# Two graph networks in one kernel: the division by relation counts and the mixtures placed two bases later, the counts' lower limit on ScalarE, and other PSUM banks in v2 and the output projection

## The chip, the cores and the metric

The kernel runs on one core of a Trainium2 chip, in 32-bit floating point throughout. The metric is the device time of one execution in microseconds; lower is better. TensorE is called PE here, VectorE DVE, ScalarE ACT, GpSimd POOL, and SyncE SP, as in the profile.

## The reference, cut to what matters

There are 384 nodes with 1024 features, and 12,672 edges.

```
h = relu(layernorm(x));  x = x + attention(h)      # 16 heads, mask from the edges
h = relu(layernorm(x));  x = x + relational(h)

attention: q, k, v = linear(h); q2, k2, v2 = linear(q), linear(k), linear(v)
           softmax(q2 k2^T / 8 + mask) v2, then a linear map (the output projection)
relational (D = 768, R = 6 relations, B = 4 bases, L = 2 layers):
  x = relu(h w_in + b_in)
  per layer:  W_r = sum_b comp[r,b] basis[b]
              out[n] = sum over edges (s -> n, type r) of (x W_r)[s] / counts[r, n]
                       + x root + bias
              x = batchnorm(relu(out) + x)
  layernorm(x w_out + b_out)
```

`counts[r, n]` is the number of edges of type r that end in n.

## The kernel before

**Edges to dense matrices.** POOL scatters edge values into tables in device memory: the mask values into `mtab` (L261) and the edge counts into `atab` (L266, an indirect DMA that adds). The four mask tables are read back and merged on DVE into the tile `mask8` (L306 to L320). These steps are a generator, `edge_steps`; `fill(n)` runs n steps of it between pieces of other work. The count tables are read into `A`, six relations of 384 x 384 (L830 to L837): two loads on SP and the rest on POOL, where a second table is accumulated into each relation by DMA. `add_up(r)` sums a relation's three row tiles on POOL.

**Attention.** After q, k and v, the product v2 is made in halves by `v_products`, a scheme with fewer multiplications and more additions, in banks of PSUM that `vbanks` names. The last third of the rows is made by `second_v(half)` (L562), which stands between the first score products (L701). `exponents(g)` reads the scores and `mask8` on DVE, then ACT takes the exponential. The output projection is at L789 to L826; its last rows are two plain products at L818 to L823, with `relu_T` (transposes of the normalised rows) between them.

**Relational layers.** For each layer and basis b, PE computes H_b = X basis_b (L950 to L992): three pieces c = 0, 1, 2, then products of sums (`times`), each read from PSUM by ACT or DVE. One product, `rest`, is left over and done after piece 0 of the next basis. Behind the four bases comes X root (L994 to L1001), then At times H (from L1057 on), where

    At_b = sum_r comp[r,b] * A_r / counts_r

`share(r)` (L340) divides: PE adds up `sums[r]` over the partitions with a matrix of ones (L343), DVE limits the count to at least 1, takes the reciprocal and multiplies `A[:, r]`; it then starts `add_up(r + 4)`. `mix(l, r, At, bs)` (L324) adds relation r into At for the bases `bs`, on ACT for r = 0 and on DVE otherwise. The table `between` (L932) says after which piece of which basis each is called: the key is (layer, basis, piece), where piece 4 is the end of a basis and basis 4 is the root product. Bases are counted from 0 here: the third and fourth are 2 and 3.

**What sets the order.** The order of every engine is that of the program (`manual_schedule`). PSUM has 8 banks, and `next_bank(name, among)` takes the bank that was handed out longest ago among those allowed:

```
i = next(i for i in ring if i in among)
ring.remove(i)
ring.append(i)
```

A product into a bank waits until what the bank held was read. Weights go through `wload`, five buffers and SP's queue. A basis needs three loads; the third of the next basis and two of the one after start as the current basis lets go of its buffers.

Of the kernel before, what the change touches and what calls it, by code (L numbers as in the profile page):

```python
# [10 lines left out]
F32 = mybir.dt.float32  # L11
# [6 lines left out]
P = 128  # L18
# [33 lines left out]
def gnn_kernel(ctx: ExitStack, tc: tile.TileContext, out, x, edges, chunks, cols, rows, small,  # L52
# [14 lines left out]
    def bank(i, name):  # L67
        return psum.tile([P, 512], F32, tag=f"bank{i}", name=name)

    def next_bank(name, among=range(8)):  # L70
# [4 lines that stand above are left out]
        return bank(i, name)  # L75
# [45 lines left out]
    nc.vector.tensor_scalar(ident, jp, 0.0, None, ALU.is_equal)  # L121
    ones = const.tile([P, P], F32, name="ones")
    nc.gpsimd.memset(ones, 1.0)

    hT = keep.tile([P, KD, N], F32, tag="hT", name="hT")

# [46 lines left out]
    def edge_steps(ep, none, zero):  # L173
# [129 lines left out]
        for i in range(EC - PER + DEALT):  # L303
            put_count()
            if i == 1:
                V = [mask8] + [ep.tile([P, NT, N], F32, tag=f"V{j}", name=f"V{j}") for j in range(1, MT)]  # L306
                for v, tab in zip(V, mtab):
                    nc.gpsimd.dma_start(v, tab[:MCELLS, :].rearrange("(t p d) o -> p t (d o)", p=P, t=NT))
                for j, v in enumerate(V[1:]):
                    if j == 1:  # L310
                        yield
                    given = ep.tile([P, NT, N], F32, tag="given", name="given")
                    nc.vector.tensor_scalar(given, v, 4.0 * NEG, None, ALU.is_gt)
                    nc.vector.copy_predicated(mask8, given.bitcast(I32), v)

                for n in range(NT):
                    blk = mask8[:, n, n * P:(n + 1) * P]
                    bare = ep.tile([P, P], F32, tag="bare", name="bare", bufs=2)
                    nc.vector.scalar_tensor_tensor(bare, blk, 4.0 * NEG, ident, ALU.is_lt, ALU.mult)
                    nc.vector.copy_predicated(blk, bare.bitcast(I32), sp[:, 2, 3:4].to_broadcast([P, P]))  # L320
# [10 lines left out]
                nc.vector.scalar_tensor_tensor(At[:, b], A[:, r], w, At[:, b], ALU.mult, ALU.add)  # L331

    sums = {}

    def add_up(r):
        sums[r] = late.tile([P, N], F32, tag="sum", name="sum", bufs=4)
# [2 lines left out]

    def share(r):  # L340

        ps = next_bank("ps_cnt", ring[1:])
        nc.tensor.matmul(ps[:, :N], ones, sums[r], start=True, stop=True)  # L343
        rn = late.tile([P, N], F32, tag="rn", name="rn", bufs=2)
        nc.vector.tensor_scalar(rn, ps[:, :N], 1.0, None, ALU.max)
        nc.vector.reciprocal(rn, rn)
        nc.vector.tensor_tensor(A[:, r], A[:, r], rn[:, None, :].to_broadcast([P, NT, N]), ALU.mult)
        if r + 4 < R:
            add_up(r + 4)


    with ExitStack() as inner:
# [68 lines left out]
        with tc.tile_pool(name="edge", bufs=1, side="right") as ep:  # L421
# [131 lines left out]

            v2 = ap.tile([P, NT, D], F32, tag="T", name="v2", bufs=4)
            VT = [output_weights(half) for half in range(2)]
            vbanks = [[bank(i, "ps_v2") for i in range(3)], [next_bank("ps_v2", (4, 5, 6, 7)) for _ in range(3)]]

            def v_out(half, i, j):
                c = half * 512 + j * 256
# [1 line left out]

            def second_v(half):  # L562

                ps = next_bank("ps_v2", (4, 5, 6, 7))
                for k in range(KD):
                    nc.tensor.matmul(ps, v[:, k, 2 * P:], wv2[half][k // 4][:, k % 4, :],
                                     start=(k == 0), stop=(k == KD - 1))
                return lambda: nc.scalar.copy(v2[:, 2, half * 512:(half + 1) * 512], ps)
# [4 lines left out]
            def v_products(half):  # L573

                pa, pb, pc = [ps[:, :256] for ps in vbanks[half]]
                T1, T2, T3, T4 = VT[half]
                multiply(pa, va(0, 0), vb(half, 0, 0), True)
                nc.scalar.copy(v_out(half, 0, 0), pa)
                yield
                multiply(pb, va(0, 1), vb(half, 1, 0), True)  # L580
                add_out(half, 0, 0, pb)
                yield
                multiply(pc, VS[0], T1, True)
                nc.scalar.copy(v_out(half, 1, 1), pc)
                yield
                multiply(pa, VS[1], T2)
                nc.scalar.copy(v_out(half, 0, 1), pa)
                yield
                multiply(pc, VS[3], vb(half, 1, 1))
                add_out(half, 0, 1, pc)  # L590
                yield
                pd = bank(3, "ps_v2")[:, :256] if half == 0 else next_bank("ps_v2", (4, 5, 6, 7))[:, :256]
                multiply(pd, va(1, 1), T4, True)
                multiply(pa, VS[2], T3)

                def last():
                    nc.scalar.copy(v_out(half, 1, 0), pa)
                    add_out(half, 1, 1, pa)
                    add_out(half, 1, 0, pd)

                yield last
# [5 lines left out]
            next(first)()  # L607
            for _ in range(3):
                next(second)
            fill(1)  # L610
            next(second)()
            fill(1000)
        late = ctx.enter_context(tc.tile_pool(name="late", bufs=1, side="right"))
        soft_stack = ExitStack()
        soft = soft_stack.enter_context(tc.tile_pool(name="soft", bufs=1, side="right"))
# [200 lines left out]
        T4 = keep.tile([P, 4, HN], F32, tag="mask8", name="T4")  # L816

        for j in range(2):  # L818
            ps = next_bank("ps_y")[:, :256]
            for k in range(KD):  # L820
                nc.tensor.matmul(ps, attT[:, k, 2 * P:], w_o[1][k // 4][:, k % 4, j * 256:(j + 1) * 256],
                                 start=(k == 0), stop=(k == KD - 1))
            add_y(2, 512 + j * 256, ps)  # L823
            if j == 0:
                for t in range(2):
                    relu_T(h2T, t, xn[:, t, :], (0, 1))  # L826
# [60 lines left out]
    with tc.tile_pool(name="conv", bufs=1) as cp:  # L887
# [38 lines left out]
        def shares(*rs):  # L926
            return lambda: [share(r) for r in rs]

        def mixes(l, r, *bs):
            return lambda: mix(l, r, At, bs)  # L930

        between = {(0, 1, 0): shares(0), (0, 1, 1): shares(1), (0, 1, 2): lambda: mix(0, 0, At),  # L932
                   (0, 1, 4): mixes(0, 1, 0, 1), (0, 2, 0): shares(2), (0, 2, 2): shares(3),
                   (0, 2, 4): mixes(0, 2, 0, 1), (0, 3, 0): shares(4), (0, 3, 1): shares(5),
                   (0, 3, 4): lambda: [mix(0, r, At, (0, 1)) for r in (3, 4, 5)],
                   **{(0, 4, r): mixes(0, r, 2, 3) for r in range(1, R)},
                   (1, 0, 0): mixes(1, 0, 0, 1, 2, 3)}
        for i in range(10):
            between[1, (i + 1) // 3, (i + 1) % 3] = mixes(1, 1 + i // 2, *((0, 1), (2, 3))[i % 2])
# [7 lines left out]
        for l in range(L):  # L947
# [2 lines left out]
            rest = lambda: None  # L950
            for b in range(B):
                hs = [[H_[:, b, n, i * HC:(i + 1) * HC] for i in range(2)] for n in range(NT)]
                pe, pf, pb, pc, pa = [next_bank("ps_g")[:, :N] for _ in range(5)]
                kept = ring[-2:]

                def times(ps, x, y, start=False):

                    for c in range(3):
                        nc.tensor.matmul(ps, x[:, c], y(c), start=start and c == 0, stop=(c == 2),  # L959
                                         skip_group_check=not start)  # L960

                for c in range(3):
                    for ps, n, i, o, first in ((pa, 0, 0, 0, True), (pe, 2, 0, 0, True), (pf, 2, 0, 1, True),
                                               (pb, 0, 1, 0, True), (pe, 2, 1, 0, False), (pf, 2, 1, 1, False)):
                        nc.tensor.matmul(ps, block(XT, n, i)[:, c], w[c][:, i, o * HC:(o + 1) * HC],  # L965
                                         start=(first and c == 0), stop=(c == 2 and (i == 1 or ps is pa)))
                    if c == 0:
                        rest()
                        T4 = last_sums(w, T[1])
                    go_between(l, b, c)  # L970
                nc.scalar.copy(hs[0][0], pa)
                nc.vector.tensor_tensor(hs[0][0], hs[0][0], pb, ALU.add)
                times(pc, S[:, 0], lambda c: T[0][:, c], True)
                nc.scalar.copy(hs[2][0], pe)
                nc.scalar.copy(hs[2][1], pf)
                nc.scalar.copy(hs[1][1], pc)
                times(pa, S[:, 1], lambda c: T[1][:, c])
                nc.scalar.copy(hs[0][1], pa)
                times(pc, S[:, 3], lambda c: w[c][:, 1, HC:])
                nc.vector.tensor_tensor(hs[0][1], hs[0][1], pc, ALU.add)  # L980
                times(pa, S[:, 2], lambda c: T[2][:, c])
                nc.vector.tensor_tensor(hs[1][1], hs[1][1], pa, ALU.add)

                def rest(pa=pa, X=XT, T4=T4, dst=hs[1][0]):
                    times(pa, block(X, 1, 1), lambda c: T4[:, c])
                    nc.scalar.copy(dst, pa)

                if b + 1 < B:
                    w = load_basis(l, b + 1)
                    T = weight_sums(w)  # L990
                go_between(l, b, 4)
# [249 lines left out]
```

## Time and profile before

| | |
|---|---|
| median of 3 runs (lowest, highest) | 738.69 us (736.06, 740.8) |
| the profiled execution: its own time | 741.77 us |
| its span, first to last instruction | 740.0 us |
| mean granted clock of PE in it | 0.984 |
| busy in the span: PE, DVE, POOL, ACT | 705.5, 519.0, 309.6, 150.6 us |
| instructions: PE, DVE, POOL, ACT | 3228, 1313, 236, 348 |
| output projection ends, first product of h2T | 357.88 us from the start |
| basis 0, 1, 2, 3 of layer 0 begin on PE | 387.7, 407.0, 440.8, 463.4 |
| root product of layer 0, then At H begin on PE | 486.0, 511.1 |

A line of a timeline gives the start in us, the duration, the engine, the line of the kernel, the operation, the tiles out<-in, how often, and in brackets the idle time before and what ended it. A matmul in 32-bit floats appears as two instructions. A line of waits gives who waited for whom, the total in us, how often, and the longest. A row of windows gives the stretch and its length, then the busy time of PE, weight load, DVE, ACT and POOL with counts, then the granted clock of PE (1 is full), the DMA engines' share and GB/s.

### The profile page before, as it was taken

Reading aid. Unit: us, or ns where it says so; the run is one execution under the profiler, and the core shown is the slowest. Engines: PE = TensorE matmul, PEld = TensorE weight load, DVE = VectorE, ACT = ScalarE, POOL = GpSimd, SP = SyncE. Lnnn points to the kernel's source line nnn. Section 1 sums busy time; section 2 is a strip of 40 time slices with the busy share of each in tenths; the row PEclk is TensorE's granted clock in tenths of the full one; section 3 lists DMA queues with packets and bytes.
Section 4 is the critical chain, followed back from the end, with each engine's and each line's share of the span. In section 5 each row is a group of like instructions: output and inputs, shape, how many; then the busy total and the mean of one; then the engine's idle time right before and its main releaser. Section 6 shows DMA issues by size and latency. Waiting matters only on the chain.

```text
span 740.0 us, 8821 instructions
## 1 busy us (share of the span) xinstructions
PE 705.5 (95%) x3228; PEld 530.0 (72%) x3228; DVE 519.0 (70%) x1313; ACT 150.6 (20%) x348; POOL 309.6 (42%) x236
## 2 busy tenths in 40 slices
PE   8999999999995999997999689999999999999995
PEld 8759999999983444476995355557995555579943
DVE  6877796869774799775524559989679776506755
ACT  4202112111110577410131031101113111001100
POOL 1466767866887677587786471000000000030000
PEclk9999999999998999998999899999999999999999
DMA  8797787256424522633424993241002223610001
GB/s 296 255 369 219 227 243 209 39 198 202 116 57 129 170 2 1 214 43 44 85 1 66 256 245 87 114 171 43 11 33 76 73 108 128 240 58 1 1 28 57
DMA packets 40536, 91.00 MB, mean 123 GB/s; under 512 B 19644, under 2 KB 27680, under 8 KB 36270
## 3 DMA queue, kind: packets, MB, share of 16 engines
q1 hardware_dynamic: 18478, 79.62, 30.7%
q0 software_dynamic: 21008, 8.42, 10.4%
q10 hardware_dynamic: 1008, 2.41, 0.8%
q8 instruction: 25, 0.41, 0.2%
q14 instruction: 17, 0.14, 0.1%
HBM read 79.27 MB, written 11.16 MB: 122 GB/s over the span
## 4 chain that ended last, share of the span: by engine, by line
PE 64%; POOL 17%; DMA 11%; issue 6%; DVE 1%; ACT 0%; DVEq 0%; POOLq 0%
POOL atab L266 13%; PE ps_c L1057 11%; PE ps_g L965 10%; PE ps_k L382 10%; PE ps_g L959 9%; DMA atab<-count,at 8%; PE ps_c L999 6%; PE ps_q L400 6%; PE ps_q L382 5%; PE ps_f L1163 4%; POOL mtab L261 3%; DMA A<-atab 2%; PE ps_v L382 2%; DMA x_sb<-in_x 1%; DVE st L136 1%
## 5 line engine op out<-in xcount | busy, mean ns | idle before, releaser
L266 POOL DMA_INDIRECT atab<-count,at x99 | 164.7, 1664 | 58.8 <-DMA atab<-count,at 34.4
L261 POOL DMA_INDIRECT mtab<-m_val,at x99 | 106.9, 1080 | 57.2 <-issue 26.8
L1150 POOL TENSOR_TENSOR x_sb<-x_sb,room 128x1024 f32<-128x1024 f32 x3 | 7.0, 2349 | 194.0 <-DMA room<-in_rows 194.0
L331 DVE SCALAR_TENSOR_TENSOR At<-A,small_sb,At 128x1152 f32<-128x1152 f32 x40 | 53.7, 1413 | 0.0
L959 PE MATMUL ps_g<-T,S 128*128 128x384 f32 x144 | 49.1, 486 | 0.0
L965 PE MATMUL ps_g<-w_c,XT 128*128 128x384 f32 x144 | 48.9, 494 | 0.0
L965 PE MATMUL ps_g<-w_c,XN 128*128 128x384 f32 x144 | 47.6, 486 | 0.0
L400 PE MATMUL ps_q<-hT,w_q 128*128 128x384 f32 (+1 forms) x160 | 41.8, 422 | 1.4 <-ACT hT L90 1.4
L965 PEld LDWEIGHTS ps_g<-w_c,XT 128*128 128x128 f32 x144 | 28.0, 195 | 19.7 <-issue 1.5
L959 PEld LDWEIGHTS ps_g<-T,S 128*128 128x128 f32 x144 | 27.4, 190 | 19.1
L965 PEld LDWEIGHTS ps_g<-w_c,XN 128*128 128x128 f32 x144 | 27.3, 190 | 18.8
L400 PEld LDWEIGHTS ps_q<-hT,w_q 128*128 128x128 f32 x160 | 28.5, 190 | 14.1 <-ACT hT L90 1.7
L1087 DVE TENSOR_TENSOR XN<-XN,ps_c 128x192 f32<-128x192 f32 x38 | 12.6, 349 | 34.4 <-ACT XN L1043 19.7
L1057 PE MATMUL ps_c<-At,H 128*128 128x192 f32 x216 | 36.4, 326 | 0.0
L1057 PEld LDWEIGHTS ps_c<-At,H 128*128 128x128 f32 x216 | 35.4, 190 | 0.5
L382 PE MATMUL ps_k<-T,S 128*128 128x192 f32 x192 | 35.2, 327 | 0.5 <-ACT k L498 0.5
L382 PEld LDWEIGHTS ps_k<-T,S 128*128 128x128 f32 x192 | 31.8, 190 | 0.8 <-ACT k L498 0.8
L1163 PE MATMUL ps_f<-w_out,XN 128*128 128x512 f32 (+1 forms) x84 | 31.1, 531 | 0.0
L250 DVE SCALAR_TENSOR_TENSOR same<-keys,key,weigh 128x128 f32<-128x128 int32 x99 | 28.0, 346 | 1.2 <-DVE same L250 1.2
L250 DVE SCALAR_TENSOR_TENSOR same<-cells,own,later 128x128 f32<-128x128 int32 x99 | 27.9, 348 | 0.4
L656 DVE CUSTOM_DVE_ANT_0 s<-ps_s,mask 128x384 f32<-128x384 f32 x48 | 24.5, 549 | 5.0 <-PE ps_s L643 4.8
L1163 PEld LDWEIGHTS ps_f<-w_out,XN 128*128 128x128 f32 x84 | 15.9, 190 | 14.9 <-issue 14.3
(295 smaller groups left out, 1418.9 us busy)
## 6 DMA issues: line engine op xcount, KB each, us to landing
w_c<-in_basis SPq DMA_DIRECT2D x24, 768.0 KB
atab<-zero SPq DMA_DIRECT2D x12, 576.0 KB
A<-atab POOLq DMA_DIRECT2D x10, 576.0 KB
w_c<-in_root SPq DMA_DIRECT2D x6, 768.0 KB
w_q<-in_wq SPq DMA_DIRECT2D x4, 1024.0 KB
w_q<-in_wiq SPq DMA_DIRECT2D x4, 1024.0 KB
w_k<-in_wk SPq DMA_DIRECT2D x4, 1024.0 KB
w_k<-in_wik SPq DMA_DIRECT2D x4, 1024.0 KB
```

The source lines that it names most:

```text
L250: nc.vector.scalar_tensor_tensor(same, row[:, n, :], mine[:, c:c + 1], times, ALU.is_equal, ALU.mult, accum_out=count[:, i, c:c + 1])
L261: nc.gpsimd.indirect_dma_start(mtab[c // PER][:, :], bass.IndirectOffsetOnAxis(at[:, 0, c:c + 1], 0), m_val[:, c:c + 1], None)
L266: nc.gpsimd.indirect_dma_start(atab[0 if i < 18 - DEALT else i % 2][:, :], bass.IndirectOffsetOnAxis(at[:, 1, c:c + 1], 0), count[:, 1, c: ...
L331: nc.vector.scalar_tensor_tensor(At[:, b], A[:, r], w, At[:, b], ALU.mult, ALU.add)
L382: nc.tensor.matmul(ps, a[:, k, :], b[:, k, :], start=start and k == 0, stop=(k == 3), skip_group_check=not start)
L400: nc.tensor.matmul(ps[o][:, c], wt_[:, k, o * P:(o + 1) * P], src[:, k, c], start=(k == 0 and c.start == 0), stop=(k == KD - 1 and c.stop ...
L656: nc.vector.tensor_tensor_reduce(s[j], ps[:, :N], mask8[:, t, :], -scale, 3.0e38, ALU.add, ALU.min, tops[:, j:j + 1])
L959: nc.tensor.matmul(ps, x[:, c], y(c), start=start and c == 0, stop=(c == 2), skip_group_check=not start)
L965: nc.tensor.matmul(ps, block(XT, n, i)[:, c], w[c][:, i, o * HC:(o + 1) * HC], start=(first and c == 0), stop=(c == 2 and (i == 1 or ps is ...
L999: nc.tensor.matmul(pr[o], w[k // 2][:, k % 2, o * P:(o + 1) * P], XT[:, k, :], start=(k == 0), stop=(k == KC - 1))
L1057: nc.tensor.matmul(ps, x[:, c], y[:, c], start=start and c == 0, stop=stop and c == 5, skip_group_check=True)
L1163: nc.tensor.matmul(p, XT[:, k, t * P:(t + 1) * P], w[k // 2][:, k % 2, c0:c1], start=(k == 0), stop=(k == KC - 1))
```

## The change

- The shares leave basis 1 of layer 0 for bases 2 and 3; all mixtures of r = 1 to 5 are made at the end of basis 3, and those of r = 0 in pairs behind share 2 and share 3.
- The limit of the counts at 1 is computed on ACT as relu(count - 1) + 1, with a new constant tile `minus`.
- `share` takes a bank that the current basis doesn't use (`taken`), and a basis doesn't take the bank of the `rest` before it.
- In v2 the second half's banks are fixed to 4, 5, 6 and 7, and `second_v` uses 5 and 6. The merging of the mask tables is no longer cut by a `yield`, and stands ahead of the last additions of v2.
- The first plain product of the output projection's last rows takes any bank but 0.

```diff
+    minus = const.tile([P, 1], F32, name="minus")
+    nc.gpsimd.memset(minus, -1.0)
...
-                for j, v in enumerate(V[1:]):
-                    if j == 1:
-                        yield
+                for v in V[1:]:
                     given = ep.tile([P, NT, N], F32, tag="given", name="given")
...
+    taken = []
...
     def share(r):
-        ps = next_bank("ps_cnt", ring[1:])
+        ps = next_bank("ps_cnt", [i for i in range(8) if i not in taken])
         nc.tensor.matmul(ps[:, :N], ones, sums[r], start=True, stop=True)
         rn = late.tile([P, N], F32, tag="rn", name="rn", bufs=2)
-        nc.vector.tensor_scalar(rn, ps[:, :N], 1.0, None, ALU.max)
+        nc.scalar.activation(rn, ps[:, :N], AF.Relu, bias=minus)
+        nc.scalar.activation(rn, rn, AF.Identity, bias=ones[:, 0:1])
         nc.vector.reciprocal(rn, rn)
...
-            vbanks = [[bank(i, "ps_v2") for i in range(3)], [next_bank("ps_v2", (4, 5, 6, 7)) for _ in range(3)]]
+            vbanks = [[bank(i, "ps_v2") for i in range(3)], [next_bank("ps_v2", (i,)) for i in (4, 5, 6)]]
...
-                ps = next_bank("ps_v2", (4, 5, 6, 7))
+                ps = next_bank("ps_v2", (5 + half,))
...
-                pd = bank(3, "ps_v2")[:, :256] if half == 0 else next_bank("ps_v2", (4, 5, 6, 7))[:, :256]
+                pd = bank(3, "ps_v2")[:, :256] if half == 0 else next_bank("ps_v2", (7,))[:, :256]
...
-            fill(1)
+            fill(1000)
             next(second)()
-            fill(1000)
...
-            ps = next_bank("ps_y")[:, :256]
+            ps = next_bank("ps_y", range(1, 8))[:, :256]
...
-        between = {(0, 1, 0): shares(0), (0, 1, 1): shares(1), (0, 1, 2): lambda: mix(0, 0, At),
-                   (0, 1, 4): mixes(0, 1, 0, 1), (0, 2, 0): shares(2), (0, 2, 2): shares(3),
-                   (0, 2, 4): mixes(0, 2, 0, 1), (0, 3, 0): shares(4), (0, 3, 1): shares(5),
-                   (0, 3, 4): lambda: [mix(0, r, At, (0, 1)) for r in (3, 4, 5)],
-                   **{(0, 4, r): mixes(0, r, 2, 3) for r in range(1, R)},
+        between = {(0, 2, 0): shares(0), (0, 2, 1): shares(1),
+                   (0, 2, 2): lambda: [share(2), mix(0, 0, At, (0, 1))],
+                   (0, 2, 4): lambda: [share(3), mix(0, 0, At, (2, 3))],
+                   (0, 3, 0): shares(4), (0, 3, 1): shares(5),
+                   (0, 3, 4): lambda: [mix(0, r, At) for r in range(1, R)],
                    (1, 0, 0): mixes(1, 0, 0, 1, 2, 3)}
...
-                pe, pf, pb, pc, pa = [next_bank("ps_g")[:, :N] for _ in range(5)]
+                pe, pf, pb, pc, pa = [next_bank("ps_g", [i for i in range(8) if i not in taken[-1:]])[:, :N]
+                                      for _ in range(5)]
+                taken[:] = ring[-5:]
```

## The prediction

> **What bounds the kernel now.** I read the page's busy rows first: PE is at work in 95% of the span of 740.0 us (705.5), the next engine, DVE, in 70%. So only PE's idle time can be won, and the waits of PE alone list nearly all of it.
>
> ```profile
> PE ps_cnt L343 <- POOL sum L338: 8.9, 2, 6.9
> PE ps_v L566 <- DVE v L571: 7.9, 1, 7.9
> PE ps_y L821 <- DVE x_sb L784: 4.4, 1, 4.4
> PE ps_q L400 <- ACT hT L90: 1.4, 1, 1.4
> ```
>
> Three waits hold 21.2 us, and the change touches exactly these three. Next the windows around them; the first column after POOL is PEclk, the granted clock.
>
> ```profile
> 236.00:238.00 2.00, 1.83 (x2) 0.84 (x3) 1.97 (x4) 0.78 (x1) 0.55 (x1) 0.50 0.08 9
> 348.00:350.00 2.00, 2.00 (x6) 1.61 (x5) 0.00 (x0) 0.00 (x0) 1.69 (x2) 0.50 0.25 0
> 420.00:423.00 3.00, 3.00 (x5) 1.79 (x6) 1.33 (x2) 0.00 (x0) 0.00 (x0) 0.50 0.73 274
> ```
>
> After each of the three waits PE runs at half clock, so a wait costs more than its idle time. The timelines of PE, DVE, ACT and POOL show what must be ready:
>
> ```profile
> 346.59 6.26 PE L821 MATMUL ps_y<-w_o,attT 128*128 128x256 f32 x16 [4.40 <-DVE x_sb L784]
> ...
> 354.43 3.62 PE L821 MATMUL ps_y<-w_o,attT 128*128 128x256 f32 x16
> ```
> ```profile
> 233.37 0.96 DVE L313 TENSOR_SCALAR given<-V 128x1152 f32<-128x1152 f32 x1 [9.49 <-DMA V<-mtab]
> ...
> 242.79 0.56 DVE L656 CUSTOM_DVE_ANT_0 s<-ps_s,mask 128x384 f32<-128x384 f32 x1 [0.18 <-DVE mask L320]
> ...
> 486.61 21.35 DVE L331 SCALAR_TENSOR_TENSOR At<-A,small_sb,At 128x1152 f32<-128x1152 f32 x16
> ```
> ```profile
> 427.55 4.69 ACT L329 ACTIVATE At<-A,small_sb 128x1152 f32<-128x1152 f32 x4 [14.04 <-DVE A L347]
> ```
> ```profile
> 452.50 1.00 POOL L337 TENSOR_TENSOR sum<-A 128x384 f32<-128x384 f32 x1 [8.93 <-DMA A<-atab]
> ```
>
> The same 16 matmuls of L821 take 6.26 us after the wait and 3.62 without. The mask is the other thing to see: DVE gets the mask tables at 233.37 and can only begin the softmax at 242.79.
>
> **What the Trainium skill says.** "TensorE: Matmul & The Clock Gate", What's actually happening: the array falls to half clock after an idle window of some 3.4 us and needs about as long to come back. The trace agrees: 0.50 after idle times of 7.9, 4.4 and 6.9 us. The same page, Architectural detail, calls ACT's queue strictly first in, first out; the ACT timeline keeps program order. "ScalarE: Activation LUTs", Table sets: relu and identity are in every set, so the new activations should load no table; this trace has Relu and Identity side by side at L864 to L872 with no load. "DMA: Bandwidth & Descriptors", Queues, rings and completion order: the engines share themselves between the queues by packets. The trace agrees in that the accumulate into A issued at 438.5 landed at 452.5 (14 us) with three weight loads (issued from 437.75) beside it, and the one of 428.3 at 436.5 (8 us) without.
>
> **The change part by part**, against the execution of 741.77 us (span 740.0 and 1.8 around it). It is 3.1 us above the median of the runs, 738.69; I take the sum off the median.
>
> *Output projection.* The first L821 product gets a bank other than 0 (by the ring, 2), which was read long ago. It starts when L695 ends, 342.2, not at 346.59, and takes 3.5 us at full clock: done 345.7. The ring then gives bank 0 to the first transpose of relu_T, which waits for the addition that ends at 346.54: 0.9 us. Transposes 1.75 to 348.4, second product 3.5 to 351.9, where before the next matmul (first_products) came at 357.88. **Minus 6.0.** DVE is ready: the last xn is normalised at 345.9.
>
> *v2.* second_v(0) takes bank 5, read long ago, so the wait of 7.9 before it goes. What is late next is the softmax. scores(2), just behind second_v(0) on PE, needs the banks that exponents(0) reads, and these need the mask. Moving the last v2 additions (0.73) behind the rest of the mask work only reorders DVE, so exponents(0) stays at 242.79. PE does second_v(0) from 228.3 to 235.4, then idles 8 us until 243.4 and is cold again: scores(2), scores(3) take up to 3 us instead of 1.6. second_v(1) comes between 245.2 (no cold) and 246.5 (all cold), before at 246.17. So between minus 0.9 and plus 0.4; I take **0**.
>
> *Shares leave basis 1.* From its first matmul at 407.03 to that of basis 2 at 440.79 are 33.8 us; basis 2 with two share products took 22.6, so a bare basis is 22.6 less 2 x 0.65 = 21.3. The two products are done later, so 33.8 - 21.3 - 1.3 = **minus 11.2**, of which 8.9 was idle and 2.3 the cold clock. This needs sums ready at the new places. PE is 6 ahead, so basis 1 begins at 401.2 and basis 2 at 422.5; share 0 comes at 428.4 (sum ready 419.9), share 1 at 433 (428.4), share 2 at 437.5 (432.5), share 3 at 448 (438.6), 4 and 5 at 455 and 460 (443.6, 454.6). Every sum is early by 4.6 us or more; that is the cover.
>
> *Lower limit on ACT.* It removes 6 DVE instructions of 0.55 and adds 12 on ACT of about 0.52 (row of L1090). ACT is busy 20%; the reciprocal starts some 0.5 us later each time, and no PE instruction waits for it: 0.
>
> *share(2), then two mixtures on ACT, at the end of the matmuls of basis 2.* Behind them on ACT stands the copy of pa (L971), and pa's next product waits for that copy. Let t be the end of those matmuls. The count product ends t+0.65, two activations t+1.8, two mixtures of 1.17 (4.69/4) t+4.2, the copy t+4.7. PE has only the count product and pc's (1.94) until t+2.6. **Plus 2.1.** Before, the four mixtures ran ahead of that point (427.55 to 432.2) and PE never waited. The pair after share(3) hides behind the next basis' first 3.9 us of matmuls.
>
> *Banks.* By the ring, share(4) gets the bank that rest() has just filled, so its product waits for one ACT copy of 0.48: **plus 0.7** with the hand-over. All other new banks were read long before.
>
> *Mixtures behind basis 3.* 20 on DVE now follow basis 3, before 16 (486.61 to 507.96, 1.334 each): 5.3 us more. After them come four sums of At, four of H and take(0,0), which frees the bank for PE's product of 520.84; take ended 517.03, a slack of 3.8. 5.3 - 3.8 = 1.5, **plus 1.6** with the hand-over. q(0,0) itself is in time: 18 mixtures end 24 us after basis 3, PE gets there after 25.2.
>
> Sum: -6.0 - 11.2 + 0 + 2.1 + 0.7 + 1.6 = -12.8. 738.7 - 12.8 = **725.9**.
>
> *Unknown: DMA.* In basis 1, part 2 of its weights is issued on SP only behind A's loads (402.08), so at about 403, no earlier than 1 us before now; it had landed by 410.6 and PE needs it at 410.9. The next three loads move from 437.75 to about 419.5, into the loads and accumulates of A. Taking over the 6 us (14 less 8) that an accumulate lost beside loads, share 2, with 4.6 of slack, would stall by 1.4; bounds 0 and 6 (all of it, repeated at share 1). I take 0, since the loads thereby leave the later accumulates alone.
>
> **Rivals.**
> 1. *All costs hidden*: ACT's mixtures and the longer DVE tail find slack that I don't see, and second_v(1) comes 0.9 earlier. -17.2 - 0.9 = -18.1: 720.6. Against it: the ACT order is fixed.
> 2. *Weights and accumulates collide* as bounded above, with a cold clock after the stall (up to 2.3): -12.8 + 6 + 2 = -5: 734.
> 3. *The sums become the bound* (the other side). POOL issues each accumulate only after the load before it, so a delay of 6 us could repeat at each of relations 2 to 5: sum 5 at 454.6 + 24 = 478.6 against a need at 460, a stall of 18.6 and 2 cold. -12.8 + 20.6 = +7.8: 746.5. It decides once sum 5 is later than about 472 (12.8 less the cold 2 beyond 460), three full delays. Against it: the three loads are one burst of 2.4 MB, gone in 6 us at the 386 GB/s of 420 to 422.
> 4. *The chain on POOL sets the end*: the page's chain runs through POOL's scatters until the first sum, so PE's gains before 420 would turn into waiting at share 0. That holds if share 0 stood where it was; it now comes 8.5 us after its sum. If this cover failed, 6.0 goes back and the shares' gain shrinks: about 738, no change.
>
> **How the numbers follow.** My forecast, net -9 to -16 (722.5 to 729.5): 0.60. Rival 1: 0.12. Rival 2: 0.17. Rival 3: 0.05. Rival 4: 0.06. 1% is 7.4 us, about what a measurement of this kernel can tell from no change. Faster by more: 0.60 + 0.12 + half of rival 2 = 0.80; within: half of rival 2 and rival 4 = 0.15; slower: 0.05. The range leaves out the fast end of rival 1 and rivals 3 and 4: 721 to 734; the likeliest case alone is 722.5 to 729.5.
>
> **What would show it.** In the new profile: the waits of PE no longer list L343 <- POOL sum; L821 has two equal groups of 3.5; L566 has no wait, but an idle time of about 8 appears at L643 <- DVE s; a wait of about 2 at L959 on ACT H L971 in basis 2; one of 1 to 2 at L1057 on DVE L1087 in layer 0; no table load at share. I am wrong if PE waits at L343 for POOL, at L965 for a weight load, or gains its 7.9 at v2 after all.

## The result, and the profile after

| | before | after |
|---|---|---|
| median (lowest to highest, runs) | 739.42 (736.06 to 740.8, 4) | 729.05 (727.74 to 731.59, 4) |
| profiled execution; its span | 741.77; 740.0 | 731.59; 729.8 |
| PE busy | 705.5 | 702.7 |

The ratio is 0.987, 95% interval 0.9826 to 0.9915: faster by 1.3%, some 10 us. In a later series the changed kernel was measured again beside the kernel before and gave 0.9913 (0.9872 to 0.9953), some 6 us. Medians here count every execution; the ratios leave out those more than 1.5% above the fastest of their kernel. In four profiles, called late ones below, PE was busy for 93 to 104 of the 120 us from 100 to 220, against 119 in the profile before; only waits behind that stretch are read from them.

The waits of PE in the changed kernel (who waited for whom, us in total, times, longest):

```profile
PE ps_s L646 <- DVE top L659: 7.9, 1, 7.9
PE ps_g L964 <- ACT H L976: 2.0, 1, 2.0
...
PE ps_g L970 <- DVE XN L1092: 1.1, 1, 1.1
PE ps_h L165 <- DVE x_sb L787: 1.0, 1, 1.0
PE ps_c L1062 <- DVE XN L1092: 0.8, 1, 0.8
PE ps_cnt L345 <- ACT H L991: 0.7, 1, 0.7
```

The waits of 8.9 and 4.4 are gone. The one of 7.9 is not: it stands at the score products (L646) and no longer at v2. Five waits of 0.7 to 2.0 are new. PE's timeline shows what each costs behind itself:

```profile
241.32 3.40 PE L646 MATMUL ps_s<-k,q 64*128 64x384 f32 x8 [7.86 <-DVE top L659]
244.65 8.07 PE L570 MATMUL ps_v<-w_v,v 128*128 128x512 f32 x16
...
341.18 3.62 PE L824 MATMUL ps_y<-w_o,attT 128*128 128x256 f32 x16
345.75 1.97 PE L165 MATMUL ps_h<-ident,xn 128*128 128x128 f32 x16 [0.95 <-DVE x_sb L787]
347.56 3.62 PE L824 MATMUL ps_y<-w_o,attT 128*128 128x256 f32 x16
...
441.05 3.89 PE L964 MATMUL ps_g<-T,S 128*128 128x384 f32 x6 [2.04 <-ACT H L976]
```

Eight score instructions take 3.40 behind the wait where they take 1.56 at full clock, and the second v2 product 8.07 where it takes 7.13. The output projection's two products are equal now, 3.62 each. At 441.05 six matmul instructions took 3.89, which take 2.10 everywhere else in this profile: half clock again, behind a wait of only 2.04. The windows there have the granted clock in the last column but two:

```profile
243.00:244.00 1.00, 1.00 (x5) 0.43 (x3) 1.00 (x3) 1.00 (x5) 0.98 (x1) 0.50 0.06 0
...
443.00:444.00 1.00, 1.00 (x3) 0.61 (x2) 0.27 (x1) 0.00 (x0) 0.66 (x1) 0.50 1.14 200
```

Basis 1 has no share product left and no wait. Its first matmuls and those of basis 2, before and after:

```profile
407.03 4.03 PE L965 MATMUL ps_g<-w_c,XT 128*128 128x384 f32 x12
...
440.79 4.03 PE L965 MATMUL ps_g<-w_c,XT 128*128 128x384 f32 x12
```
```profile
400.14 4.03 PE L970 MATMUL ps_g<-w_c,XT 128*128 128x384 f32 x12
...
421.43 4.03 PE L970 MATMUL ps_g<-w_c,XT 128*128 128x384 f32 x12
```

On DVE, the softmax and the mixtures behind basis 3:

```profile
240.71 0.55 DVE L659 CUSTOM_DVE_ANT_0 s<-ps_s,mask 128x384 f32<-128x384 f32 x1
...
473.44 26.67 DVE L332 SCALAR_TENSOR_TENSOR At<-A,small_sb,At 128x1152 f32<-128x1152 f32 x20
```

**Where the time went.** The softmax can start only when the mask is merged, and that moment moved from 242.79 to 240.71 in these two executions. POOL had issued the loads of the mask tables 2.0 sooner too (224.62 instead of 226.60), and the second profile of the changed kernel has the softmax at 244.93, later than before the change. So this 2.1 is taken for chance. From it to the end of the execution there are 741.77 - 242.79 = 499.0 us before and 731.59 - 240.71 = 490.9 after: minus 8.1. In the second profile, with the mask at 244.93, the time was 736.01: 491.1, the same. The stretches (from PE's timelines, start to start) sum to it:

| stretch | before | after | difference | predicted |
|---|---|---|---|---|
| softmax begins to scores(4) on PE | 10.45 | 11.94 | +1.5 | 0 |
| to first_products | 104.64 | 98.36 | -6.3 | -6.0 |
| from first_products through basis 0 to basis 1 | 49.15 | 49.13 | 0 | 0 |
| basis 1 | 33.76 | 21.29 | -12.5 | -12.5 |
| basis 2, with two more count products | 22.57 | 27.86 | +5.3 | +3.4 |
| basis 3 | 22.58 | 23.47 | +0.9 | +0.7 |
| root product to the product with T2 (pa) | 34.90 | 36.46 | +1.6 | +1.6 |
| to the first product of layer 1 | 31.20 | 32.54 | +1.3 | 0 |
| layer 1 and the end | 189.73 | 189.83 | +0.1 | 0 |

### The profile page after: what moved, and what is told of

Its sections match the earlier page's. It is cut to its first block, busy times and chain, and to the rows that moved or that the text cites. A ratio compares the mean times of both kernels' runs of the same rounds, so it can differ in the third digit from the quotient of the medians.

```text
span 729.8 us, 8833 instructions
## 1 busy us (share of the span) xinstructions
PE 702.7 (96%) x3228; PEld 527.9 (72%) x3228; DVE 514.3 (70%) x1307; ACT 157.7 (22%) x360; POOL 309.6 (42%) x237
## 3 DMA queue, kind: packets, MB, share of 16 engines
q0 software_dynamic: 21008, 8.42, 10.4%
## 4 chain that ended last, share of the span: by engine, by line
PE 71%; DVE 12%; DMA 6%; POOL 6%; issue 3%; ACT 2%; DVEq 0%; POOLq 0%; ACTq 0%
PE ps_g L970 13%; PE ps_g L964 10%; PE ps_c L1062 9%; PE ps_q L404 6%; PE ps_q L386 5%; PE ps_k L386 5%; PE ps_f L1168 4%; POOL mtab L264 4%; DVE At L332 4%; PE ps_y L386 3%; PE ps_c L1004 3%; DMA mtab<-m_val,at 3%; PE ps_x L386 3%; PE ps_o L691 2%; PE ps_s L646 2%
## 5 line engine op out<-in xcount | busy, mean ns | idle before, releaser
L964 PE MATMUL ps_g<-T,S 128*128 128x384 f32 x144 | 51.0, 500 | 2.0 <-ACT H L976 2.0
L1092 DVE TENSOR_TENSOR XN<-XN,ps_c 128x192 f32<-128x192 f32 x38 | 12.5, 349 | 30.8 <-ACT XN L1048 19.7
L646 PE MATMUL ps_s<-k,q 64*128 64x384 f32 x96 | 23.4, 559 | 7.9 <-DVE top L659 7.9
L985 DVE TENSOR_TENSOR H<-H,ps_g 128x384 f32<-128x384 f32 x8 | 4.4, 555 | 35.0 <-PE ps_g L964 35.0
```

Source lines behind the costliest of these rows:

```text
L646: nc.tensor.matmul(score[g][j][:, :N], q2[ho, hc, t * P:(t + 1) * P], k2[ho, hc, :], start=True, stop=True)
```

## The experiments

Each was timed beside the kernel before on its chip; "ratio" is to that. A difference below some 3 us can't be read from these times, so the verdicts on parts of that size rest on lines of the profiles.

**One part alone.** Three kernels take one part each, a fourth leaves one out.

```diff
# a_out_bank: the kernel before and
-            ps = next_bank("ps_y")[:, :256]
+            ps = next_bank("ps_y", range(1, 8))[:, :256]
# b_shares: the change without that line and without v2
# c_v2: the kernel before with the banks and the fill of v2
# d_no_v2: the change without these
```

> The kernel before with one edit: the first plain product of the output projection's last rows takes any bank but 0. Theory (gains before the shares count only if the shares no longer wait for POOL): first_products follows 6.0 us sooner behind the scores, but share 0, still in basis 1, waits for its sum, so the wait at L343 grows from 6.9 to some 13 and the time stays within 1 us of 739.4. Rival (the three gains are independent): minus 6.0, 733.4.

Measured: 739.14, ratio 0.9962 (0.9925 to 0.9999), some 3 us, between the two expectations. The profile is a late one: PE reached the first scores at 246.28 instead of 226.74. So late, it met sums that were ready, and there was no wait at L343 to grow. It still ended 5.0 us sooner than the profile of before (736.79 against 741.77): the lead that it lacked is what the kernel before spends on its waits for the mask and the sums. Its two products at L821 take 3.62 each. That the gain needs the shares to be free of POOL is neither shown nor refuted by this run: it holds only for executions in which PE is ahead of POOL. The times of this series speak for it: d_no_v2 is b_shares plus this same edit, and from 0.9959 to 0.9869 are 6.7 us (4.1 to 9.3), where the edit alone gave 2.8 (0.1 to 5.5). The two intervals overlap, so this is a sign and no proof. The profile shows something else:

```profile
426.27 2.10 PE L959 MATMUL ps_g<-T,S 128*128 128x384 f32 x6
429.91 2.20 PE L959 MATMUL ps_g<-T,S 128*128 128x384 f32 x6 [1.54 <-ACT H L971]
```

With the sums on time, the kernel before has a wait on ACT of its own, behind its four mixtures of relation 0 (in c_v2, late too, 2.11). The wait for the sums had covered it.

> The change without its bank in the output projection and without the v2 part: shares, mixtures, taken and the limit on ACT alone. Theory: minus 11.2 for the shares, plus 3.8 at the ACT mixtures (2.0 of wait and 1.8 at half clock), 0.8 for the bank of share 4, 1.6 for the mixtures' tail, 1.2 at the start of layer 1: minus 3.8, 735.6. Rival (the costs of these parts come from the other edits' earlier arrival): minus 11, 728.

Measured: 738.41, ratio 0.9959 (0.9934 to 0.9984), minus 3: the theory's number, and the rival's minus 11 is out. Its profile, a late one, has the waits of 2.0 (ACT), 1.1 (layer 1), 0.8 (mixtures' tail) and 0.7 (bank of share 4) of the whole change, so they belong to this part. The half clock that the theory put behind the first is not there:

```profile
472.56 2.20 PE L967 MATMUL ps_g<-T,S 128*128 128x384 f32 x6 [2.04 <-ACT H L979]
```

> The kernel before with the v2 part alone. Theory: PE's idle time of 7.9 us moves from in front of second_v(0) to in front of scores(2), and the half clock moves with it onto more work: from exponents(0) on DVE to scores(4) on PE it takes 11.9 us instead of 10.5. The end does not move (739.4 within 1 us), since share 0 waits for POOL all the same. Rival (the 7.9 are won): scores(4) comes 7 us sooner after exponents(0), about 3.5 us; the end may still not move.

Measured: 738.9, ratio 0.9995 (0.9968 to 1.0022). The end doesn't move, as expected; on the move of the idle time its profile, a late one, says nothing, since PE came to the first scores 28 us after that of before and did not wait for the mask.

> The changed kernel without its v2 part. Theory: exponents(0) to scores(4) goes back from 11.9 to 10.5 us and nothing later swallows it: 1.4 faster than the changed kernel, some 727.6. Rival (the v2 part is a small gain, or nothing): 729 to 730, and 11.9 stays.

Measured: 734.35, ratio 0.9869 (0.9844 to 0.9893), not to be told from the changed kernel: the interval is 3.6 us wide and the two expectations differ by 1.4 to 2.4. Its profile is a late one as well. Inconclusive. That v2 costs 1.5 is thus read from profiles alone, the two of the changed kernel and that of f_limit_dve against the one of before, and no run without the v2 part confirms it.

**The wait on ACT.** Two kernels take its two suspects apart.

```diff
# e_mix_early
-        between = {(0, 2, 0): shares(0), (0, 2, 1): shares(1),
-                   (0, 2, 2): lambda: [share(2), mix(0, 0, At, (0, 1))],
+        between = {(0, 2, 0): shares(0), (0, 2, 1): lambda: [share(1), mix(0, 0, At, (0, 1))],
+                   (0, 2, 2): shares(2),
# f_limit_dve
-        nc.scalar.activation(rn, ps[:, :N], AF.Relu, bias=minus)
-        nc.scalar.activation(rn, rn, AF.Identity, bias=ones[:, 0:1])
+        nc.vector.tensor_scalar(rn, ps[:, :N], 1.0, None, ALU.max)
```

> The changed kernel with the first two mixtures of relation 0 on ACT placed behind share 1 instead of share 2. Theory (the mixtures in front of the copy of pa cost a wait of 2.0 us and then 1.8 us of half clock): both go, the six matmuls after the copy take 2.1 again and not 3.9, basis 3 begins 3.8 sooner after basis 2; 3.8 less than the changed kernel, some 725.3. Rival (the half clock belongs to the place, not to the wait): the wait goes, the 3.9 stay, 2.0 less.

Measured: ratio 0.988 (0.9811 to 0.9949), too wide to tell; its profiled execution took 725.02. In it the twelve instructions are in one piece, at full clock:

```profile
433.58 0.81 PE L345 MATMUL ps_cnt<-sum,ones 128*128 128x384 f32 x2
434.23 4.05 PE L964 MATMUL ps_g<-T,S 128*128 128x384 f32 x12
```

From share 0 to share 4 are 24.71 us (424.55 to 449.26), in the changed kernel 28.69 (427.23 to 455.92): 4.0 less, the theory's 3.8. The half clock went with the wait; that it doesn't belong to the place is seen as well from b_shares, d_no_v2 and g_clear, which have the wait and no half clock.

> The changed kernel with the lower limit back on DVE, one instruction. Theory (of the wait on the copy of pa, 1.2 us are the two new activations in front of the mixtures): the wait of 2.0 shrinks to 0.8, and the mixtures' tail is as before the edit; 1 to 2.5 less than the changed kernel. Rival (DVE then falls behind by 0.55 a share): nothing won.

Measured: 726.48, ratio 0.9847 (0.9815 to 0.9879), beside 0.9913 for the changed kernel in the same series. The wait is gone altogether, not shrunk to 0.8. ACT's timeline shows why, first in the changed kernel, then in this one:

```profile
437.11 0.58 ACT L348 ACTIVATE rn<-ps_cnt,minus 128x384 f32<-128x384 f32 x1 [3.29 <-PE ps_cnt L345]
437.72 0.61 ACT L349 ACTIVATE rn<-rn,ones 128x384 f32<-128x384 f32 x1
438.24 2.39 ACT L330 ACTIVATE At<-A,small_sb 128x1152 f32<-128x1152 f32 x2
440.54 0.46 ACT L976 COPY H<-ps_g 128x384 f32<-128x384 f32 x1
```
```profile
432.08 2.40 ACT L330 ACTIVATE At<-A,small_sb 128x1152 f32<-128x1152 f32 x2 [5.56 <-DVE A L350]
434.39 0.46 ACT L975 COPY H<-ps_g 128x384 f32<-128x384 f32 x1
```

In the changed kernel the first new activation waits for the count product, and behind it the mixtures wait too, though their data were ready: DVE had done relation 0's division at 433.9, ACT stood idle for 3.29. With the limit on DVE nothing on ACT waits for the count, and the mixtures run 2.8 us ahead of the count product at 434.88. So it is not the time of the two activations (1.2) that costs 2.0 of wait, but that they hold up what stands behind them. Either edit alone takes the wait away: it needs both, the activations and two mixtures behind them in front of the copy. At the scores this profile has a wait of 4.39 with 3.40 and 8.09 behind it, the same price as behind 7.86.

**Layer 1.**

```diff
# g_clear
         for l in range(L):
+            taken.clear()
```

> The changed kernel with the list of taken banks emptied at the start of a layer. Theory (the list still names a bank of layer 0, so the first product of layer 1 gets the bank that DVE reads last): the wait of 1.1 at the first matmul of layer 1 goes, 1.2 less. Rival (it waits for the normalised data): the wait stays.

Measured: ratio 0.9896 (0.985 to 0.9942); profiled execution 726.49. The wait is gone:

```profile
534.81 2.11 PE L1063 MATMUL ps_c<-At,H 128*128 128x192 f32 x12
536.76 8.55 PE L971 MATMUL ps_g<-w_c,XN 128*128 128x384 f32 x26
```

So layer 1 waited because `taken` still named a bank from layer 0: the ring passed over that one, and the first product got the bank that DVE had read last. The same profile has the ACT wait of 2.04 without half clock behind it:

```profile
438.97 2.20 PE L965 MATMUL ps_g<-T,S 128*128 128x384 f32 x6 [2.04 <-ACT H L977]
```

Behind the same wait of 2.04 the six instructions took 3.89 and 3.90 in the two profiles of the changed kernel and 3.40 in the next run, but 2.20 here, in b_shares and in d_no_v2: half clock in three of six. Whether so short a wait costs the clock differs from execution to execution.

**The idle time in front of the softmax.**

```diff
# h_both_v
-            put_v = second_v(f // 2)
+            if f == 0:
+                puts = [second_v(half) for half in range(2)]
...
-            put_v()
+            puts[f // 2]()
```

> The changed kernel with both products second_v ahead of the third and fourth scores. Theory (PE's idle time before scores(2) is free room): second_v(1) runs in it, the wait shrinks from 7.9 to some 1 and the clock stays full, so scores(4) follows exponents(0) after about 3 us and not 12. Of the 9 us about 4 are kept, since the weights of basis 1 that stand behind A's loads on SP land too late for a PE that is 9 us ahead: 4 to 5 less than the changed kernel, some 725. Rival (DVE bounds the start of the softmax anyway): 0 to 1 less.

Measured: 737.09, ratio 0.9883 (0.9855 to 0.9912); no gain over the changed kernel in the times. In the profile the move did what it should where it stands:

```profile
233.16 14.00 PE L570 MATMUL ps_v<-w_v,v 128*128 128x512 f32 x32
247.09 3.04 PE L646 MATMUL ps_s<-k,q 64*128 64x384 f32 x12
```

Softmax began late here, at 245.34, and PE came out of both products only after it: no wait at scores(2), and scores(4) 3.3 us behind the softmax's start (the third group of the 3.04), not 11.9. The wait on the weights of basis 1 came as expected, 2.2. From the softmax's start to the end are 732.84 - 245.34 = 487.5 us, 3.4 less than the changed kernel's 490.9. The theory's 4 to 5 are thus nearly there from the mask on, in this one profile, but not in the times.

**Everything together.** The first version of it has all of the above except the limit on DVE, keeps the shares off the bank of the rest, and moves some of relation 1's mixtures forward.

> All of it: both second_v early, relation 0's first mixtures behind share 1, relation 1's mixtures behind share 2 and share 5 (so 16 and not 20 stand at the end), the taken list emptied per layer and the bank of the rest kept from the shares. Theory: 4 to 5 for v2, 3.8, 1.2, 0.8 and 1.5: 11 to 12 less than the changed kernel, 717 to 718. Rival (the parts hide behind one another, since the sums on POOL then set the pace): 5 to 7 less, 722 to 724.

Measured: 723.82, ratio 0.9786 (0.975 to 0.9821): short of the theory, and the rival's number. The rival's reason is not seen: PE has no wait for a sum. It has one of a new kind instead:

```profile
444.64 4.14 PE L972 MATMUL ps_g<-w_c,XT 128*128 128x384 f32 x12 [2.03 <-DVE H L987]
```

The two mixtures behind share 2 (3.48 us) kept DVE from the addition that frees a bank for basis 3. Hence:

```diff
# k_best, against i_best
-                   (0, 2, 2): lambda: [share(2), mix(0, 1, At, (0, 1))],
+                   (0, 2, 2): shares(2),
-                   ... (0, 3, 2): mixes(0, 1, 2, 3),
-                   (0, 3, 4): lambda: [mix(0, r, At) for r in range(2, R)],
+                   ... (0, 3, 2): mixes(0, 1, 0, 1),
+                   (0, 3, 4): lambda: [mix(0, 1, At, (2, 3))] + [mix(0, r, At) for r in range(2, R)],
# l_best_pool, against k_best
-            nc.sync.dma_start(A[:, r], tabs[1][r])
+            nc.gpsimd.dma_start(A[:, r], tabs[1][r])
```

> As the run of everything together, but relation 1's first two mixtures stand behind piece 2 of basis 3 and no longer behind share 2, so 18 mixtures are left for the end. Theory (the two mixtures of 1.4 on DVE delayed the additions that free a bank for basis 3): the wait of 2.0 at the first matmul of basis 3 on DVE H goes, no wait appears at the start of At times H, and the time falls by some 2 to 721 to 722. Rival (it only hid another wait): the wait moves, nothing is won, 723.8.

Measured: 720.45, ratio 0.9748 (0.97 to 0.9795). The wait on DVE H is gone and none stands at At times H. The softmax began late in this profile (246.38), and PE, at the first scores at 227.82, waited 3.68 for it even with both products ahead. By the times alone the gain over the first version can't be told, as the two intervals overlap.

> The same with A's first two loads issued on POOL and not on SP, so the weights of basis 1 don't stand behind them. Theory: where PE is early, the wait on w_c in basis 1 (2.2 in the run with both products early) goes; 0 to 2 less than the same without. Rival: A's loads and the weights then land together and the first sum comes later; 0.

Measured: 717.98, ratio 0.972 (0.9681 to 0.976); not to be told from the one before it. Neither profile has a wait on w_c, so what A's loads on POOL are worth is not shown. All waits of PE in the last one:

```profile
PE ps_q L404 <- ACT hT L90: 1.4, 1, 1.4
PE ps_warm L132 <- POOL ones L123: 1.3, 1, 1.3
PE ps_o L691 <- ACT attT L694: 1.1, 1, 1.1
PE ps_h L165 <- DVE x_sb L788: 0.9, 1, 0.9
PE ps_x L386 <- DVE XT L867: 0.4, 1, 0.4
PE ps_s L646 <- DVE top L659: 0.4, 1, 0.4
```

This version beats both kernels: 5.5 us of wait in all. From the softmax's start to its end are 715.14 - 237.65 = 477.5 us, against 490.9 and 499.0.

**The changed kernel again.**

> The changed kernel itself, unchanged, for a second profile and more times. If it depends on the execution how early PE reaches the softmax, then this profile has either the wait of 7.9 at scores(2) with 3.4 and 8.1 behind it, or no wait with 1.6 and 7.1; the ratio stays at 0.987.

Measured: 734.53, ratio 0.9913 (0.9872 to 0.9953). The interval just misses 0.987; it overlaps that of the first series (0.9826 to 0.9915). Its profile has the wait (8.85) with 3.40 and 8.23 behind it, as the first had; the profiles of e_mix_early and g_clear, whose v2 is the same, have no wait, with 1.56 and 7.13. There PE came to the first scores at 232.7 and the softmax began at 238.8; here 228.06 and 244.93.

## Why the prediction was right, and where its sizes were off

The mechanism was right in its main parts, and 725.9 against 729.05 is some 3 us too low. Part of the agreement is luck: in the later series the gain was 6.4 us (3.5 to 9.5), half of the 12.8 forecast and outside the likeliest case of 9 to 16. In both profiles of the changed kernel the gain from the softmax on is 8 against the one profile of before, and the rest hangs on when the mask is merged.

- **Output projection** (minus 6.0): the two products are 3.62 each and the wait of 0.95 for bank 0 is there. The stretch lost 6.3, of which 0.2 to 0.3 lies in the attention.
- **Shares leave basis 1** (minus 11.2): 33.76 to 21.29 with the products moved, to the tenth. No sum was waited for. The unknown was there: relation 2's accumulate and the loads met, and POOL waited 6.20 where before it had no such wait at that sum:

```profile
418.22 1.30 POOL L836 DMA_DIRECT2D A<-atab  x1 [3.25 <-DMA A<-atab]
...
430.65 0.99 POOL L339 TENSOR_TENSOR sum<-A 128x384 f32<-128x384 f32 x1 [6.20 <-DMA A<-atab]
```

  Issue to sum took 12.4 us instead of 6.7. It cost PE nothing: sum 2 was ready at 432.7 and needed at 436.3. So the value taken, 0, was right with 3.6 us to spare, but some of that is luck, as A's loads began 3.8 us sooner in this execution (398.31 on SP). In the second profile of the changed kernel they began at 406.33, the same step took 9.2, and 3.0 were to spare (437.7 and 440.7). Rivals 2, 3 and 4 did not occur. (The mark of about 472 in rival 3 is 470.8 by its own sum; nothing hangs on it.)
- **v2** (0, between minus 0.9 and plus 0.4): **mis-sized, plus 1.5.** The idle time moved to the scores as foretold. But half clock cost 1.84 on the scores and 0.94 on the second product, 2.8, where before it cost 8.58 - 7.13 = 1.45. I had let the clock come back when the scores were done; it came back at about 246.5, some 5 us after PE's restart at 241.32 and not the 3 of the wait before (236.17 to about 239.1).
- **share(2) and the ACT mixtures** (plus 2.1): **mis-sized.** The wait is 2.04, the copy where I had put it, but in both profiles of the changed kernel 1.8 of half clock came behind it: 3.9. I had priced the clock for the long waits only. And the reason was half right: f_limit_dve shows that without the new activations ACT does the mixtures before the count product. The step "lower limit on ACT: 0", whose cover was that no PE instruction waits for the reciprocal, looked at what comes after the activations and not at what stands behind them on ACT. Together with the place of the mixtures it cost the 3.9. (The activations loaded no table, as foretold, and took 0.58 and 0.61 where I had taken 0.52.)
- **Banks** (plus 0.7): 0.66 of wait at share 4, right; **but "all other new banks were read long before" failed** at layer 1: the ring was followed to the names of the banks, not to who reads them last there. Plus 1.3; g_clear takes it away.
- **Mixtures behind basis 3** (plus 1.6): 1.6, in two waits of 0.34 and 0.78 and their hand-overs.

The three mis-sized terms are 1.5 + 1.8 + 1.3 = 4.6; the forecast from the softmax on would have been -12.8 + 4.6 = -8.2, and the trace has -8.1. That the median's -10.4 is larger because the mask came earlier in those runs, and the second series smaller because it came later, fits the two profiles; the other executions have none. The moment itself follows POOL: over the ten profiles that are not late ones the softmax begins at 237.5 to 246.4, and each time 16.1 to 18.4 us after POOL issues the first load of the mask tables (L308 before). What moves that issue was not tried.

## What to carry to other kernels

What an instruction moved to an idle engine costs is to be sought in what stands behind it in that engine's order and in how long it waits at the head, and not only in its own duration: here two activations of 0.6 us held up 2.4 us of other work. A wait that is removed from one place should be followed along the program to the next instruction with the same dependency before it is counted; here the softmax's mask held both. And a wait of PE can have a second price, the half clock behind it, even where it is only 2 us long.

## What was not expected of the hardware

A wait of 2.04 us was enough to halve PE's clock behind it in three profiles (3.89, 3.90 and 3.40 instead of 2.10), and not in three others with the same wait (2.20). The Trainium skill, "TensorE: Matmul & The Clock Gate", What's actually happening, gives half clock after at least one idle window of some 3.4 us; here less was enough. It also calls the window free-running. That would make the moment of a wait matter and not only its length, which fits three against three, but no run here tests it.

Nor need a PE that comes late lose by it. In e_mix_early, with PE at the first scores at 232.7 instead of 224.8, no wait arose and so no half clock. There scores(4) began at 249.8, 2.8 us sooner than in the changed kernel's profile (252.65), though the softmax began only 1.9 sooner.
